# Pairwise bilinear products: W in one packed buffer with half-width loads, chunks aligned at their ends, one transposed x

## The chip, the cores and the metric

The kernel runs on one core of a Trainium2 chip. The metric is the device time of one execution in microseconds (us); of several executions the median is taken. Engines are called by the names of the profile: PE is TensorE (matmuls), PEld its weight loads, DVE is VectorE, ACT is ScalarE, POOL is GpSimd, SP is SyncE, which here only issues DMAs. A "tile" in this document is a tile of 128 batch rows unless it says otherwise.

## The reference

There are F = 32 fields of D = 64 features for each of 4,096 batch rows. For each of the 496 pairs of fields i < j there is one matrix W of 64 x 64. The output of a pair is field i times W, multiplied element by element with field j:

```python
i_idx, j_idx = np.triu_indices(32, k=1)
vi = inputs[:, i_idx, :]
vj = inputs[:, j_idx, :]
vdotw = jnp.einsum('bpd,pde->bpe', vi, W)
inter = vdotw * vj
return inter.reshape(B, -1)
```

All is float32. x is 33.6 MB, W 8.1 MB without padding, the output 520 MB.

## The kernel before, in words

The batch is cut into 32 tiles of 128 rows (the loop over t, L122). In each tile the 32 fields are taken as 16 pairs of neighbours: p stands for the fields 2p (even) and 2p + 1 (odd). Field i has `width[i]` = (31 - i) x 64 output columns, one 64-column block for each later field.

x of a tile is loaded by one DMA on ACT's queue (`load_x`, L80 to 83) into one of two buffers. PE needs it transposed, features on partitions: `transpose_x` (L97) makes eight 128 x 128 transposes into two PSUM banks and one ACT copy of them to xT. One xT tile holds all 16 pairs; for pair p, the even field lies on partitions 0 to 63 and the odd field on partitions 64 to 127. There are two xT buffers. The two halves of the next tile's xT are made at the pairs 5 and 6 of this tile (`PREFETCH_AT`, L133 to 136), ahead of those pairs' matmuls in PE's order.

W lies in HBM as 128 rows: rows 0 to 63 for even fields, rows 64 to 127 for odd fields, the odd ones padded by 64 columns so that both have the same width (16,384 columns in all). It is loaded once, by 16 DMAs on SP's queue, one per pair, each of 128 partitions, into 16 SBUF tiles (L113 to 116). The stores are issued from the same queue, behind these loads.

The products of a pair are cut into chunks of up to 512 columns from the left (L137). A chunk takes two PSUM banks out of a ring of eight (`take_banks`), one matmul goes into each (even field and odd field), and DVE multiplies both with x in one instruction of up to 1,024 columns (L155), whose sources and destination are two runs. Its x operand starts at two places, 64 columns apart, one for each field. Where the odd part is missing, or the padding would reach past the end of the group, DVE takes the two fields one by one (L164). Padding columns that L155 writes are overwritten by the following instruction.

DVE writes into a ring of 28,160 columns of SBUF. One tile has 31,744 output columns, in four groups (`STORES`): pairs 0 and 1 (7,552 columns), 2 and 3 (6,528), 4 to 6 (7,872), 7 to 15 (9,792). After each group SP issues one store of it (L170). A group that doesn't fit in the rest of the ring starts again at column 0. The first DVE instruction that writes over a part of the ring waits for the store that still reads it.

The order on each engine is the order of the program. The framework adds the waits, by the regions that are read and written, also inside one large buffer.

Of the kernel before, what the change touches and what calls it, by code (L numbers as in the profile page):

```python
# [1 line left out]

# [6 lines left out]

F32 = mybir.dt.float32  # L10
ALU = mybir.AluOpType

P = 128
BANK = 512
BANKS = 8
CHUNK = BANK

STORES = [[0, 1], [2, 3], [4, 5, 6], [7, 8, 9, 10, 11, 12, 13, 14, 15]]
PREFETCH_AT = [5, 6]
RING = 28160  # L20


@with_exitstack
def pair_bilinear_kernel(
    ctx: ExitStack,
    tc: tile.TileContext,
    x: bass.AP,
    w: bass.AP,
    out: bass.AP,
    F: int,  # L30
    D: int,
):

    nc = tc.nc
    B = x.shape[0]
    NT = B // P
    NPR = F // 2

    width = [(F - 1 - i) * D for i in range(F)]
    off = [sum(width[:i]) for i in range(F)]
    woff = [sum(width[0 : 2 * p : 2]) for p in range(NPR)]  # L60
    store_w = [sum(width[2 * p] + width[2 * p + 1] for p in g) for g in STORES]

    const = ctx.enter_context(tc.tile_pool(name="const", bufs=1))
    xtpool = ctx.enter_context(tc.tile_pool(name="xT", bufs=2))
    psum = ctx.enter_context(tc.tile_pool(name="ps", bufs=1, space=bass.MemoryType.PSUM))

    ident = const.tile([P, P], F32, tag="ident", name="ident")
    make_identity(nc, ident)

    def runs(tl, a, b, n):  # L70

        ap = tl[:, a : a + n]
        return bass.AP(ap.tensor, ap.offset, [list(ap.ap[0]), [b - a, 2], list(ap.ap[1])])


    xbuf = [const.tile([P, (F + 1) * D], F32, tag=f"x{b}", name=f"x{b}") for b in range(2)]
    for xb in xbuf:
        nc.gpsimd.memset(xb[:, F * D :], 0.0)  # L78

    def load_x(t):  # L80
        xt = xbuf[t % 2]
        nc.scalar.dma_start(out=xt[:, : F * D], in_=x[ts(t, P), :])
        return xt

    pring = psum.tile([P, BANKS * BANK], F32, tag="pring", name="pring")
    bank = 0

    def take_banks(n):

        nonlocal bank  # L90
        if bank + n > BANKS:
            bank = 0
        got = pring[:, bank * BANK : (bank + n) * BANK]
        bank = (bank + n) % BANKS
        return got

    def transpose_x(xT, t, xt, g):  # L97

        n = 2 * BANK // P
        pt = take_banks(2)  # L100
        for c in range(n):
            nc.tensor.transpose(pt[:, ts(c, P)], xt[:, ts(n * g + c, P)], ident)  # L102
        nc.scalar.copy(xT[:, ts(g, 2 * BANK)], pt)  # L103

    def new_xT(t):
        return xtpool.tile([P, NPR * P], F32, tag="xT", name=f"xT_{t}")

    ring = const.tile([P, RING], F32, tag="ring", name="ring")
    at = 0
    xs = {0: load_x(0)}  # L110

    w_sb = []
    for p in range(NPR):  # L113
        wp = const.tile([P, width[2 * p]], F32, tag=f"w{p}", name=f"w{p}")
        nc.sync.dma_start(out=wp, in_=w[:, woff[p] : woff[p] + width[2 * p]])
        w_sb.append(wp)

    xTs = {0: new_xT(0)}
    for g in range(2):
        transpose_x(xTs[0], 0, xs[0], g)  # L120

    for t in range(NT):  # L122
        xt, xT = xs.pop(t), xTs.pop(t)
        if t + 1 < NT:
            xs[t + 1] = load_x(t + 1)
        for s, group in enumerate(STORES):
            if at + store_w[s] > RING:
                at = 0
            osb = ring[:, at : at + store_w[s]]
            at += store_w[s]  # L130
            o0 = off[2 * group[0]]
            for p in group:
                if t + 1 < NT and p in PREFETCH_AT:  # L133
                    if t + 1 not in xTs:
                        xTs[t + 1] = new_xT(t + 1)
                    transpose_x(xTs[t + 1], t + 1, xs[t + 1], PREFETCH_AT.index(p))
                for c0 in range(0, width[2 * p], CHUNK):  # L137
                    n = [max(0, min(CHUNK, width[2 * p + h] - c0)) for h in range(2)]
                    half = -(-n[0] // BANK) * BANK
                    pm = take_banks(2 * half // BANK)  # L140
                    for b0 in range(0, n[0], BANK):
                        b1 = min(b0 + BANK, n[0])
                        for h in range(2):
                            if b0 < n[h]:
                                nc.tensor.matmul(  # L145
                                    pm[:, h * half + b0 : h * half + b1],
                                    xT[h * D : (h + 1) * D, ts(p, P)],
                                    w_sb[p][h * D : (h + 1) * D, c0 + b0 : c0 + b1],
                                    start=True,
                                    stop=True,  # L150
                                )
                    o = [off[2 * p + h] - o0 + c0 for h in range(2)]
                    xj = [(2 * p + h + 1) * D + c0 for h in range(2)]
                    if n[1] > half - BANK and o[1] + n[0] <= store_w[s]:
                        nc.vector.tensor_tensor(  # L155
                            runs(osb, o[0], o[1], n[0]),
                            runs(pm, 0, half, n[0]),
                            runs(xt, xj[0], xj[1], n[0]),
                            ALU.mult,
                        )  # L160
                    else:
                        for h in range(2):
                            if n[h]:
                                nc.vector.tensor_tensor(  # L164
                                    osb[:, o[h] : o[h] + n[h]],
                                    pm[:, h * half : h * half + n[h]],
                                    xt[:, xj[h] : xj[h] + n[h]],
                                    ALU.mult,
                                )
            nc.sync.dma_start(out=out[ts(t, P), o0 : o0 + store_w[s]], in_=osb)  # L170


# [33 lines left out]
```

## Time and profile before

| what | value |
|---|---|
| median of 3 runs | 1337.88 us (1337.68 to 1337.98) |
| the profiled execution's own time | 1337.58 us |
| its span (first to last instruction) | 1335.8 us |
| PE busy | 1154.1 us (86%) |
| DVE busy | 1199.1 us (90%) |
| ACT busy | 66.1 us (5%) |
| moved by DMA | 562.88 MB, 421 GB/s over the span |
| of it written to HBM | 520.09 MB |
| clock granted to TensorE | 0.971 of full speed |

The profile is of one execution. Its page shows the busy time of each engine, then the span in 40 equal slices with the busy share in tenths (9 is 90% or more), the DMA queues, and groups of instructions: line, engine, operation, destination and sources, shape and count, then busy time and the mean duration of one in ns, and last the idle time before them with what ended it. Queue q1 is SP's, q10 is ACT's. Busy times of matmuls are modelled, since matmuls are pipelined. Beside the page, the trace answers questions on waits and on single stretches of the span, and it keeps a record of each DMA packet: queue, start, duration and size.

### The profile page before, as it was taken

The numbers are of one execution on the slowest core, as the hardware profiler recorded it, in microseconds if no ns is written. First come the engines' busy times: TensorE is split into PE (matmuls) and PEld (weight loads), VectorE is DVE, ScalarE is ACT, GpSimd is POOL, SyncE is SP. The second block draws the span as 40 slices with busy tenths as digits, with TensorE's granted clock in tenths as the row PEclk, the third lists the DMA queues.
The fourth block names the chain that finished last, engine by engine and source line by source line (L and its number), as shares of the span: only waits on it lengthen the run. The fifth ranks groups of instructions, "written<-read, shape, count | busy, mean of one in ns | idle before, by whom it ended". The sixth has DMA issues, their size and how long they took to land. (4 is left out here: it accounts for less than half of the span.)

```text
span 1335.8 us, 13084 instructions
## 1 busy us (share of the span) xinstructions
PE 1154.1 (86%) x5376; PEld 529.9 (40%) x5376; DVE 1199.1 (90%) x1344; ACT 66.1 (5%) x65; POOL 0.9 (0%) x8
## 2 busy tenths in 40 slices
PE   7898898988888889898888898898988888888883
PEld 3343343433343444344334444343443333333331
DVE  5999898999899999899999899989988989999994
ACT  1000000000000000000000000000000000000000
POOL 0000000000000000000000000000000000000000
PEclk9999999899999999999999999999999999999997
DMA  9999999999999999999999999999999999999998
GB/s 392 435 426 431 436 408 434 415 426 431 419 417 425 428 429 416 418 424 420 424 436 419 418 421 426 424 426 421 418 430 414 426 423 413 424 427 430 418 420 370
DMA packets 25403, 562.88 MB, mean 421 GB/s; under 512 B 2944, under 2 KB 3328, under 8 KB 4864
## 3 DMA queue, kind: packets, MB, share of 16 engines
q1 hardware_dynamic: 20736, 528.49, 92.6%
q10 hardware_dynamic: 4608, 33.56, 6.0%
q8 instruction: 42, 0.69, 0.2%
q14 instruction: 17, 0.14, 0.0%
HBM read 41.94 MB, written 520.09 MB: 421 GB/s over the span
## 5 line engine op out<-in xcount | busy, mean ns | idle before, releaser
L155 DVE TENSOR_TENSOR ring<-pring,x 128x1024 f32<-128x1024 f32 (+3 forms) x1088 | 1154.2, 1107 | 116.9 <-DMA out_dram<-ring 68.0
L145 PE MATMUL pring<-w,xT 64*128 64x512 f32 (+4 forms) x4864 | 1087.8, 563 | 132.3 <-DVE ring L155 127.9
L145 PEld LDWEIGHTS pring<-w,xT 64*128 64x128 f32 x4864 | 472.9, 192 | 721.4 <-DVE ring L155 611.7
L103 ACT COPY xT<-pring 128x1024 f32<-128x1024 f32 x64 | 64.8, 1012 | 1197.1 <-PE pring L102 1197.1
L102 PE MATMUL pring<-ident,x 128*128 128x128 f32 x512 | 71.5, 285 | 30.7 <-DMA x<-in_x_dram 30.3
L102 PEld LDWEIGHTS pring<-ident,x 128*128 128x128 f32 x512 | 57.0, 144 | 65.6 <-issue 65.6
L164 DVE TENSOR_TENSOR ring<-pring,x 128x64 f32<-128x64 f32 (+4 forms) x256 | 70.9, 297 | 3.3
L103 ACT ACT_TABLE_LOAD x1 | 1.3, 1283 | 1.7 <-PEq L198 1.7
masks.py:199 POOL TENSOR_SCALAR_AFFINE_SELECT ident<-ident 128x128 f32<-128x128 f32 x1 | 0.3, 292 | 0.0
L78 POOL MEMSET x<- 128x64 f32 x2 | 0.2, 152 | 0.0
masks.py:197 POOL MEMSET ident<- 128x128 f32 x1 | 0.2, 204 | 0.3 <-POOLq L198 0.3
L198 POOL MEMSET const-bfloat16-1.0<- 128x1 bf16 x1 | 0.1, 101 | 0.0
L198 POOL MEMSET const-uint8-127<- 128x1 uint8 x1 | 0.1, 101 | 0.0
L198 POOL MEMSET const-float32-0.0<- 128x1 f32 x1 | 0.1, 98 | 0.2 <-issue 0.2
L198 POOL MEMSET const-float32-1.0<- 128x1 f32 x1 | 0.1, 98 | 0.0
## 6 DMA issues: line engine op xcount, KB each, us to landing
out_dram<-ring SPq DMA_DIRECT2D x32, 4896.0 KB, 18.6
out_dram<-ring SPq DMA_DIRECT2D x32, 3936.0 KB, 17.4
out_dram<-ring SPq DMA_DIRECT2D x32, 3776.0 KB, 19.0
out_dram<-ring SPq DMA_DIRECT2D x32, 3264.0 KB, 19.4
x<-in_x_dram ACTq DMA_DIRECT2D x32, 1024.0 KB, 17.8
w<-in_w_dram SPq DMA_DIRECT2D x1, 992.0 KB, 7.5
w<-in_w_dram SPq DMA_DIRECT2D x1, 928.0 KB, 11.8
w<-in_w_dram SPq DMA_DIRECT2D x1, 864.0 KB, 13.4
```

The lines of the kernel that those rows point to most:

```text
L78: nc.gpsimd.memset(xb[:, F * D :], 0.0)
L102: nc.tensor.transpose(pt[:, ts(c, P)], xt[:, ts(n * g + c, P)], ident)
L103: nc.scalar.copy(xT[:, ts(g, 2 * BANK)], pt)
L145: nc.tensor.matmul(pm[:, h * half + b0 : h * half + b1], xT[h * D : (h + 1) * D, ts(p, P)], w_sb[p][h * D : (h + 1) * D, c0 + b0 : c0 + b1 ...
L155: nc.vector.tensor_tensor(runs(osb, o[0], o[1], n[0]), runs(pm, 0, half, n[0]), runs(xt, xj[0], xj[1], n[0]), ALU.mult,)
L164: nc.vector.tensor_tensor(osb[:, o[h] : o[h] + n[h]], pm[:, h * half : h * half + n[h]], xt[:, xj[h] : xj[h] + n[h]], ALU.mult,)
L198: nc = bacc.Bacc("TRN2", target_bir_lowering=False, num_devices=1)
```

## The change

W is stored in one SBUF buffer of 16,384 columns, without the padding. In HBM the odd fields' half starts with 64 columns of zeros, and behind them the odd fields follow one another without gaps; the last 960 columns of that half are never loaded. The load is cut into five groups of pairs (`LOADS`: pair 0, pair 1, pairs 2 and 3, 4 to 6, 7 to 15), and each group into two DMAs, one for the partitions 0 to 63 and one for 64 to 127: ten DMAs of 64 partitions, with rows of 7,168 to 20,736 bytes.

Chunks are now aligned at their right end: the first chunk of a pair is the short one. The odd field's columns are counted one block further left, so that one chunk of both fields needs the same columns of x. DVE's x operand then reads one run twice (a step of 0). In the first chunk of a pair the odd field's first 64 columns are no result of it; they fall on the last block of the even field's output and are overwritten by the pair's last chunk. A pair that has a single chunk (the pairs 12 to 15) is taken field by field.

There is one xT buffer. The second half of this tile's xT is made at pair 3 of the tile, the first half of the next tile's at pair 9. Before the first tile only one half is made. The x buffers lose their 64 columns of zeros and with them two memsets.

```diff
-CHUNK = BANK
 
 STORES = [[0, 1], [2, 3], [4, 5, 6], [7, 8, 9, 10, 11, 12, 13, 14, 15]]
-PREFETCH_AT = [5, 6]
+
+LOADS = [[0], [1], [2, 3], [4, 5, 6], [7, 8, 9, 10, 11, 12, 13, 14, 15]]
+
+FIRST_HALF_AT, SECOND_HALF_AT = 9, 3
...
-    woff = [sum(width[0 : 2 * p : 2]) for p in range(NPR)]
+    woff = [i % 2 * D + sum(width[i % 2 : i : 2]) for i in range(F)]
...
-    xtpool = ctx.enter_context(tc.tile_pool(name="xT", bufs=2))
+    xT = const.tile([P, NPR * P], F32, tag="xT", name="xT")
...
-    w_sb = []
-    for p in range(NPR):
-        wp = const.tile([P, width[2 * p]], F32, tag=f"w{p}", name=f"w{p}")
-        nc.sync.dma_start(out=wp, in_=w[:, woff[p] : woff[p] + width[2 * p]])
-        w_sb.append(wp)
+    load_x(0)
+    w_sb = const.tile([P, sum(width[0::2])], F32, tag="w", name="w")
+    for g in LOADS:
+        for h in range(2):
+            a = woff[2 * g[0] + h]
+            b = woff[2 * g[-1] + h] + width[2 * g[-1] + h]
+            if h and g is LOADS[0]:
+                a -= D
+            nc.sync.dma_start(
+                out=w_sb[h * D : (h + 1) * D, a:b], in_=w[h * D : (h + 1) * D, a:b]
+            )
 
-    xTs = {0: new_xT(0)}
-    for g in range(2):
-        transpose_x(xTs[0], 0, xs[0], g)
-
+    transpose_x(xbuf[0], 0)
...
-                if t + 1 < NT and p in PREFETCH_AT:
-                    if t + 1 not in xTs:
-                        xTs[t + 1] = new_xT(t + 1)
-                    transpose_x(xTs[t + 1], t + 1, xs[t + 1], PREFETCH_AT.index(p))
-                for c0 in range(0, width[2 * p], CHUNK):
...
+                if p == SECOND_HALF_AT:
+                    transpose_x(xt, 1)
+                if p == FIRST_HALF_AT and t + 1 < NT:
+                    transpose_x(xbuf[(t + 1) % 2], 0)
+                first = (width[2 * p] - 1) % BANK + 1
+                for c1 in range(first, width[2 * p] + 1, BANK):
+                    n = first if c1 == first else BANK
+                    c0 = c1 - n
+                    odd = width[2 * p + 1] and c1 > D
+                    pm = take_banks(2)
+                    for h in range(1 + bool(odd)):
+                        a = woff[2 * p + h] + c0 - h * D
+                        nc.tensor.matmul(
+                            pm[:, h * BANK : h * BANK + n],
+                            xT[h * D : (h + 1) * D, ts(p, P)],
+                            w_sb[h * D : (h + 1) * D, a : a + n],
+                            start=True,
+                            stop=True,
+                        )
+                    xj = xt[:, (2 * p + 1) * D + c0 : (2 * p + 1) * D + c1]
+                    o = [off[2 * p + h] - o0 + c0 - h * D for h in range(2)]
+                    if odd and (c0 or c1 < width[2 * p]):
                         nc.vector.tensor_tensor(
-                            runs(osb, o[0], o[1], n[0]),
-                            runs(pm, 0, half, n[0]),
-                            runs(xt, xj[0], xj[1], n[0]),
+                            runs(osb, o[0], o[1], n),
+                            runs(pm, 0, BANK, n),
+                            bass.AP(xj.tensor, xj.offset, [xj.ap[0], [0, 2], xj.ap[1]]),
                             ALU.mult,
                         )
                     else:
-                        for h in range(2):
-                            if n[h]:
...
+                        for h in range(1 + bool(odd)):
+                            nc.vector.tensor_tensor(
+                                osb[:, o[h] + h * D : o[h] + n],
+                                pm[:, h * (BANK + D) : h * BANK + n],
+                                xj[:, h * D :],
+                                ALU.mult,
+                            )
```

## The prediction

> **What bounds the kernel now.** I read the page first: the busy shares and slices say which resource has no holes.
>
> ```profile
> span 1335.8 us, 13084 instructions
> ...
> DVE  5999898999899999899999899989988989999994
> ...
> DMA  9999999999999999999999999999999999999998
> GB/s 392 435 426 431 436 408 434 415 426 431 419 417 425 428 429 416 418 424 420 424 436 419 418 421 426 424 426 421 418 430 414 426 423 413 424 427 430 418 420 370
> DMA packets 25403, 562.88 MB, mean 421 GB/s; under 512 B 2944, under 2 KB 3328, under 8 KB 4864
> ...
> q1 hardware_dynamic: 20736, 528.49, 92.6%
> q10 hardware_dynamic: 4608, 33.56, 6.0%
> ```
>
> The DMA row has no slice below 9 before the last, and q1 (W loads and stores) with q10 (x) fill 98.6% of the 16 engines' span. VectorE (DVE) is busy for 90%. So I asked who waits for whom; each row gives the total, the times and the longest wait.
>
> ```profile
> DVE ring L155 <- DMA out_dram<-ring: 68.0, 35, 3.0
> DVE ring L155 <- PE pring L145: 16.7, 7, 13.6
> ```
>
> DVE waits about once a tile for a store to free ring space; for TensorE (PE) it waits 13.6 us at the start and 3.1 us in all the rest. The store queue is the bound. Next come stretches of the span: the W load, one steady tile (cut between two returns of DVE from that wait), and the tail after the last store's issue at 1319.3.
>
> ```profile
> 4.00:12.00 8.00, 3.46 (x16) 3.28 (x16) 0.00 (x0) 1.01 (x1) 0.00 (x0) 1.00 1.01 425
> 12.00:20.00 8.00, 7.67 (x35) 3.47 (x36) 6.28 (x6) 1.01 (x1) 0.00 (x0) 1.00 1.01 419
> 561.45:602.46 41.01, 36.63 (x171) 17.72 (x169) 37.48 (x42) 2.35 (x3) 0.00 (x0) 0.96 0.99 423
> 1319.30:1330.20 10.90, 0.00 (x0) 0.00 (x0) 0.00 (x0) 0.00 (x0) 0.00 (x0) 0.54 0.96 410
> ```
>
> The last two columns are DMA share and GB/s. The W load already runs at the rate of the steady tile, so it takes its bytes' worth of a full resource. The trace's packet records give each packet's size and duration: 300 ns for 7,936 B, 309 ns for 8,192 B, 1,448 ns for 39,168 B. That is 27.2 B/ns for one engine plus 8.2 ns a packet; 16 such engines give 435 GB/s. W's packets run from 1.75 to 28.23 us; the first store packet starts at 27.57, though the first store was issued at 24.7. Stores sit behind W in the same queue, so every microsecond that W takes longer moves all stores.
>
> One steady tile takes 41.0 us. An engine's own share is 8 packets of each store (1,448, 1,166, 1,119 and 968 ns) and 8 of x (309 ns): 40.1 us. The engine that ends last lags the others by about 3 us in each store. Others idle about 0.6 us a tile, but the last one has no hole.
>
> [...] All DMAs of the kernel before span 128 partitions, so no row here shows a half-width one[...].
>
> **The change part by part.**
>
> (1) W as ten half-width loads. Before, one engine carries 16,384 columns x 4 B x 8 rows = 524,288 B of W and 2 x 65,536 B of x: 655,360 / 27.2 = 24.1 us, plus 144 packets x 8.2 ns = 1.2, together 25.3 us; the records show 25.8 up to the first store packet. After, W has 16,384 columns in the lower half and 15,424 in the upper. Two bounds:
> Fast bound, engines limit: 31,808 x 4 B x 4 rows = 508,928 B an engine, 15,360 B less (0.56 us), and 88 data packets fewer (0.72 us): -1.3 us.
> Slow bound[...]: lower 16,384 x 4 x 64 B over 8 x 27.2 GB/s = 19.3 us; upper 15,424 likewise 18.1; 37.4 us, with 40 packet overheads 37.8. Before it was 19.3 + 1.05 = 20.3. So +17.4 us. [...]
> I take the slow side[...]: +15.6 us.
>
> (2) What a late W does to compute. DVE consumes W at 64 rows x 4 B per output column. A 1024-column product takes 1,217 ns, so 215 GB/s, about the half-width rate (218): compute waits only for whole loads. x0 shares the queues and lands some 2 us later. The largest load, pairs 7 to 15, lands near 46 us, while DVE reaches pair 7 at about 45; there it must wait anyway for store 0 (ring space), which starts at 45 and is in memory at 56. DVE then needs 12.2 us for group 7 to 15, done at 68; a store's first packet comes about 2 us after DVE's end, and the engines are free at 45 + 9.0 + 7.8 + 9.4 = 71. Hidden with about 1 us to spare; without that cover, up to 1 us more.
>
> (3) DVE's chunking, by shape:
>
> ```profile
> L155 DVE TENSOR_TENSOR ring<-pring,x 128x896 f32<-128x896 f32 x128 | 138.1, 1079 | 0.0
> L155 DVE TENSOR_TENSOR ring<-pring,x 128x640 f32<-128x640 f32 x96 | 78.5, 818 | 3.7 <-DVE ring L155 0.5
> L155 DVE TENSOR_TENSOR ring<-pring,x 128x384 f32<-128x384 f32 x96 | 52.8, 550 | 3.2
> L164 DVE TENSOR_TENSOR ring<-pring,x 128x320 f32<-128x320 f32 x32 | 15.3, 480 | 0.0
> L164 DVE TENSOR_TENSOR ring<-pring,x 128x256 f32<-128x256 f32 x32 | 13.2, 411 | 0.0
> L164 DVE TENSOR_TENSOR ring<-pring,x 128x192 f32<-128x192 f32 x32 | 11.1, 347 | 0.0
> L164 DVE TENSOR_TENSOR ring<-pring,x 128x128 f32<-128x128 f32 x32 | 8.9, 279 | 0.0
> ```
>
> Pairs 1 and 6 merge their last two products: 480 + 411 becomes 818 (-73 ns), 347 + 279 becomes 550 (-76). Pairs 12, 13, 14 split: 1,079 becomes 448 + 384 columns, 616 (1.043 ns a column between 64 and 1024) + 550 = 1,166 (+87); 818 becomes 480 + 411 (+73); 550 becomes 347 + 279 (+76). Sum +0.09 us a tile, 43 products for 42, and +0.16 in the two groups between the ring wait and the last store's issue. Cover: the lagging engine ends the third store about 3 us after the fourth store's first packet starts (0.16 against 3). Uncovered it would be 32 x 0.16 = 5 us. A source read twice (step 0) I cost at nothing; the trace has no such row, and if it cost 5% (61 ns on each of some 31 products, 1.9 us a tile) most of it would still be covered.
>
> (4) One xT, transposes at pairs 3 and 9. Matmuls and transposes keep their numbers. PE no longer waits for x at pair 5 (30.3 us in all, 8.5 of it the start), PE time that DVE never felt. What is queued behind a transpose on PE is the next products; PSUM holds four chunks, and 8 transposes take 1.09 us. The ACT copy overwrites a half whose readers stand earlier in PE's own order. The first product needs one ACT copy and 8 transposes, where 16 stood ahead of it: about 0.5 us sooner, hidden because stores wait for W. Two memsets go, hidden.
>
> (5) SP has six DMA issues fewer; x stays on ACT's queue at the same place. The tail is unchanged: stores end the kernel.
>
> Sum: 1337.58 us is the profiled execution's own time, with a span of 1335.8; the median of the runs is 1337.88, 0.3 us above it. 1337.58 + 15.6 + 0.0 to 0.5 for (2) = 1353.4; as a median I say 1353.5, +1.2%.
>
> **Rivals.** 0.2% (2.7 us) is about what a measurement of this kernel can tell from no change.
> A. [...] (chance 0.68): 1350 to 1357 with more or less overlap; slower.
> B. [...] regain half or more (0.09): 1341 to 1350; slower. [...]
> C. Not slower: an engine's own 27.2 B/ns is the limit[...], and fewer, longer packets save 1.3 us: 1336.5 (0.16; the last 0.03 of it for a gain over 2.7 us). It decides as soon as W flows at more than 8.14 MB / 23 us = 354 GB/s. [...]
> D. W is hidden or harmless, but DVE becomes the pacemaker of the ring (0.03): +5 us, 1343. Against: the 3 us of cover.
> E. [...] partial loads stall compute (0.04): above 1358.
>
> **How the numbers follow.** The likeliest is A, 1353.5. A, B and D make slower 0.80, E adds 0.04: 0.84; same 0.13; faster 0.03. A to B and D alone would leave out a little more than 2 in 10 (C, E and A's edges), so the range takes in C: 1336 to 1358; A's own is 1350 to 1357.
>
> **What would show it.** Right: W's packets of about 8 KB take near 600 ns where they took 300, GB/s in the stretch 12 to 20 falls from 419 to 220 to 260, the first store packet comes at 42 to 45 us, and from there the period is again 41.0 us. Step 3 is wrong if the period per tile grows, step 4 if DVE waits for PE by more than a few us after the start, step 2 if the DMA share has a hole between 45 and 75 us. Wrong altogether (C): W's stretch holds 419 GB/s or more and stores begin at 26 to 27 us.

## The result and the profile after

The changed kernel takes 1356.48 us (median of 4 runs, 1355.73 to 1358.39) against 1337.78 us (4 runs, 1337.66 to 1337.98): a ratio of 1.0142, 95% interval 1.0124 to 1.0159. The forecast was 1353.5 us, with a range of 1336 to 1358, and slower with a chance of 0.84. The profiled execution took 1357.03 us with a span of 1355.2 us, 19.4 us more than the span before.

The page of the kernel after, in the same rows as were shown of the page before:

```profile
span 1355.2 us, 13139 instructions
...
DVE  3698999888988888998888989889988889898894
...
DMA  9999999999999999999999999999999999999998
GB/s 226 349 432 429 436 426 423 431 424 421 422 414 421 432 425 422 414 422 423 433 419 420 420 420 439 421 413 428 427 418 421 413 424 424 414 422 432 426 419 359
DMA packets 23900, 562.64 MB, mean 415 GB/s; under 512 B 2720, under 2 KB 2720, under 8 KB 2976
...
q1 hardware_dynamic: 19232, 528.25, 92.5%
q10 hardware_dynamic: 4608, 33.56, 6.1%
```

A slice is 34 us. The whole difference stands in the first two: 226 and 349 GB/s where 392 and 435 stood; from the third on the rates are those of before. The row of busy shares says nothing of it: the DMA engines are just as "busy" with little more than half the bytes in the first slice. The kernel after moves fewer bytes (562.64 for 562.88 MB) in fewer packets (23,900 for 25,403), and takes longer.

Stretches of the span after (share and GB/s last):

```profile
4.00:12.00 8.00, 3.69 (x10) 2.07 (x10) 0.00 (x0) 1.01 (x1) 0.00 (x0) 1.00 1.03 271
12.00:20.00 8.00, 5.16 (x15) 3.32 (x16) 2.32 (x2) 0.00 (x0) 0.00 (x0) 1.00 1.06 232
20.00:28.00 8.00, 5.34 (x27) 3.89 (x25) 6.81 (x7) 0.00 (x0) 0.00 (x0) 0.91 1.03 220
28.00:36.00 8.00, 8.00 (x35) 4.76 (x31) 6.16 (x7) 1.01 (x1) 0.00 (x0) 0.88 0.95 203
36.00:44.00 8.00, 7.99 (x37) 4.36 (x36) 8.00 (x10) 0.00 (x0) 0.00 (x0) 1.00 1.08 226
561.45:602.46 41.01, 36.45 (x172) 17.23 (x170) 37.12 (x44) 2.03 (x2) 0.00 (x0) 0.96 0.99 422
```

Before, 12 to 20 us moved 419 GB/s. Here DMA moves 203 to 232 GB/s from 12 to 44 us, nearly all of it W, and the steady stretch (here the same times of the span as before, so a cut at another place of the tile) is back at 422. Who waits for whom after:

```profile
DVE ring L157 <- DMA out_dram<-ring: 107.3, 40, 4.3
DVE ring L157 <- PE pring L147: 24.9, 11, 16.8
DVE ring L165 <- DMA out_dram<-ring: 10.8, 1, 10.8
PE pring L147 <- DMA w<-in_w_dram: 10.4, 4, 2.9
```

The last row has no counterpart before: PE waits four times in the first tile for W. The third row is DVE's wait for the first store, at 46 to 57 us. DVE's waits for ring space grew, which is no cost: DVE needs less time now (1183.0 us busy for 1199.1; step 3 below says why) and waits for the same stores.

From the packet records, in us, with the mean period of a tile (last packet of the fourth store, from tile 4 to tile 30):

| | W's last packet ends | first store packet starts | period |
|---|---|---|---|
| before | 28.2 | 27.57 | 40.92 |
| after | 47.6 | 46.38 | 40.92 |

The first store comes 18.8 us later, 26 steady periods take the same time, and the span is 19.4 us longer.

### The profile page after: what moved, and what is told of

The parts are those of the page before. It is cut to its first block, busy times and chain, and to the rows that moved or that the text cites. A ratio compares the mean times of both kernels' runs of the same rounds, so it can differ in the third digit from the quotient of the medians.

```text
span 1355.2 us, 13139 instructions
## 1 busy us (share of the span) xinstructions
PE 1170.5 (86%) x5376; PEld 556.5 (41%) x5376; DVE 1183.0 (87%) x1376; ACT 66.1 (5%) x65; POOL 0.7 (0%) x6
## 2 busy tenths in 40 slices
DMA packets 23900, 562.64 MB, mean 415 GB/s; under 512 B 2720, under 2 KB 2720, under 8 KB 2976
## 4 chain that ended last, share of the span: by engine, by line
DMA 48%; DVE 38%; issue 10%; PE 3%; DVEq 0%; SPq 0%
DMA out_dram<-ring 47%; DVE ring L157 32%; DVE ring L165 5%; PE pring L147 3%; DMA w<-in_w_dram 1%; DVEq L157 0%; PE pring L105 0%; SPq L119 0%; DVEq L196 0%; DVEq L165 0%
## 5 line engine op out<-in xcount | busy, mean ns | idle before, releaser
L147 PE MATMUL pring<-w,xT 64*128 64x512 f32 (+4 forms) x4864 | 1107.6, 570 | 158.8 <-DVE ring L157 137.3
L157 DVE TENSOR_TENSOR ring<-pring,x 128x1024 f32<-128x1024 f32 (+3 forms) x1056 | 1103.8, 1107 | 143.1 <-DMA out_dram<-ring 107.3
L147 PEld LDWEIGHTS pring<-w,xT 64*128 64x128 f32 x4864 | 500.3, 195 | 722.8 <-DVE ring L157 520.3
L165 DVE TENSOR_TENSOR ring<-pring,x 128x64 f32<-128x64 f32 (+3 forms) x320 | 97.6, 355 | 11.4 <-DMA out_dram<-ring 10.8
```

Of the source, the lines that this page charges most:

```text
L147: nc.tensor.matmul(pm[:, h * BANK : h * BANK + n], xT[h * D : (h + 1) * D, ts(p, P)], w_sb[h * D : (h + 1) * D, a : a + n], start=True, st ...
L157: nc.vector.tensor_tensor(runs(osb, o[0], o[1], n), runs(pm, 0, BANK, n), bass.AP(xj.tensor, xj.offset, [xj.ap[0], [0, 2], xj.ap[1]]), ALU ...
L165: nc.vector.tensor_tensor(osb[:, o[h] + h * D : o[h] + n], pm[:, h * (BANK + D) : h * BANK + n], xj[:, h * D :], ALU.mult,)
```

## The experiments

**Half width alone, in the kernel before.** Theory A of the expectations is rival A of the forecast: W is slow because each of its loads covers one half of the partitions.

```diff
-        nc.sync.dma_start(out=wp, in_=w[:, woff[p] : woff[p] + width[2 * p]])
+        for h in range(2):
+            nc.sync.dma_start(
+                out=wp[h * D : (h + 1) * D, :],
+                in_=w[h * D : (h + 1) * D, woff[p] : woff[p] + width[2 * p]],
+            )
```

> The kernel before with each of its 16 W loads cut into two DMAs, partitions 0 to 63 and 64 to 127; nothing else is changed. If the half width is the cause (theory A[...]): W's packets take twice as long (7,936 B in 530 to 610 ns instead of 300), the first store packet comes near 46 us instead of 27.6, and the time is 1355 to 1359 us. If the packed layout, the long rows, the chunking or the single xT is the cause: 1337 to 1340 us.

Measured: 1356.38 us against 1337.86; ratio 1.0139 (1.0125 to 1.0153). The first store packet starts at 46.35 us, the period is 40.92 us. The packets of 7,936 B, the first pair's, have a median of 495 ns, a little under the 530 to 610 expected, where they took 300; those of 7,424 B, sent after them, have 553 ns, where they took 281. The stretch from 12 to 20 us:

```profile
12.00:20.00 8.00, 5.46 (x17) 2.63 (x18) 2.62 (x3) 0.00 (x0) 0.00 (x0) 1.00 1.01 225
```

This one edit gives the whole loss. Layout, row length, chunking and xT are those of before, so they aren't needed for it.

**Full width in the changed kernel.**

```diff
-        for h in range(2):
-            a = woff[2 * g[0] + h]
-            b = woff[2 * g[-1] + h] + width[2 * g[-1] + h]
-            if h and g is LOADS[0]:
-                a -= D
-            nc.sync.dma_start(
-                out=w_sb[h * D : (h + 1) * D, a:b], in_=w[h * D : (h + 1) * D, a:b]
-            )
+        a = woff[2 * g[0]]
+        b = woff[2 * g[-1]] + width[2 * g[-1]]
+        nc.sync.dma_start(out=w_sb[:, a:b], in_=w[:, a:b])
```

> The changed kernel with W loaded by five DMAs of 128 partitions, one per group of pairs, at the even fields' column bounds; layout, chunks and xT stay as changed. Theory A: packets at 26 to 27 B/ns, first store packet at 26 to 27 us, and 1336.0 to 1337.0 us, a little below the kernel before since there are fewer packets. If the rest of the change costs something (chunking on the ring's cycle, transposes): above 1338 us, with a period per tile above 40.92 us. If the layout is the cause: it stays at 1356 us.

Measured: 1338.07 us against 1337.86 (13 and 17 runs); ratio 1.0002 (0.9994 to 1.0010). The stretches of the span from 4 to 28 us:

```profile
4.00:12.00 8.00, 2.34 (x10) 1.97 (x12) 0.00 (x0) 1.01 (x1) 0.00 (x0) 1.00 1.02 430
12.00:20.00 8.00, 8.00 (x30) 3.52 (x30) 5.62 (x6) 0.00 (x0) 0.00 (x0) 1.00 1.02 434
20.00:28.00 8.00, 7.76 (x38) 3.24 (x36) 8.00 (x9) 1.01 (x1) 0.00 (x0) 1.00 1.05 419
```

DMA moves 419 to 434 GB/s again, and W's packets of 7,936 B take 300 ns. The rest of the change, all of it, is worth nothing that can be measured: period 40.94 us, first store packet at 27.37 us, 0.2 us sooner than before. The gain of 1.3 us that I had put on fewer and longer packets did not come. Of it 0.56 us can't come here, since full-width loads carry the unused columns; of the other 0.7 us, the packets' summed durations show 0.4 (25.9 us an engine for W and the first two tiles of x, 26.3 before). Why no more than 0.2 of it reached the first store was not settled. Since this version equals the kernel before within its interval, no version here beats both.

**64 partitions in the middle.** Each load is cut into three, to tell the number of partitions from their place: 64 partitions that lie half below and half above partition 64, then the two outer quarters. That the middle ones would run at the full rate was an assumption of mine that no trace had shown.

```diff
-        nc.sync.dma_start(out=w_sb[:, a:b], in_=w[:, a:b])
+        for r0, r1 in [(32, 96), (0, 32), (96, 128)]:
+            nc.sync.dma_start(out=w_sb[r0:r1, a:b], in_=w[r0:r1, a:b])
```

> As the full-width version, but each group's load is cut into three DMAs by partitions: 32 to 95, 0 to 31, 96 to 127. Theory A[...]: the DMA of 64 partitions in the middle [...] run at 26 to 27 B/ns, and those of the two outer DMAs at about 13 B/ns; W takes 9.6 + 19.3 us plus a little, the first store packet comes at 36 to 38 us, the time is 1346 to 1348 us. Rival (any DMA of 64 or fewer partitions is slow, because each engine gets only 4 rows or 2): all packets slow, 1356 us or more.

Measured: 1348.21 us, 0.2 above the range expected; ratio 1.0078 (1.0064 to 1.0092). The first store packet starts at 37.79 us. Taken in order of start, the packets of the last group show the parts: the first 64 packets of 20,736 B (the middle) have a median of 779 ns, 26.6 B/ns; the next 32 and the last 32 (the outer parts) 1,569 and 1,526 ns, 13.2 and 13.6 B/ns. The stretches hold both kinds:

```profile
12.00:20.00 8.00, 8.00 (x25) 4.84 (x25) 4.12 (x4) 0.00 (x0) 0.00 (x0) 1.00 1.03 293
20.00:28.00 8.00, 7.64 (x26) 3.19 (x24) 6.74 (x8) 0.00 (x0) 0.00 (x0) 1.00 1.03 278
```

So it isn't the number of partitions that makes a load slow, but which partitions it covers. Of 20,736 B a packet, 64 partitions from 32 on run at the full rate (779 ns; 775 for the same size at full width); 32 partitions from 0 on run at half of it (1,569 ns), as 64 from 0 on do in the kernel after (1,615 ns in the median). A limit for each side of partition 64 would fit this; the trace shows the durations, not what limits them. Half of W at half rate costs 10.2 us at the first store, a little over half of the 18.8.

**Both halves at once, from two queues.**

```diff
-            nc.sync.dma_start(
+            (nc.scalar if h else nc.sync).dma_start(
                 out=w_sb[h * D : (h + 1) * D, a:b], in_=w[h * D : (h + 1) * D, a:b]
             )
```

> The changed kernel with the upper halves of W (partitions 64 to 127) issued from ACT's queue and the lower halves from SP's, so that each engine has a packet of both halves to choose from. If engines go through both queues in step (all on one half at a time): no gain, 1354 to 1358 us. If an engine's two queues overlap[...]: W regains most of its rate, first store packet at 27 to 33 us, 1337 to 1343 us. [...] I expect 1350, between the two and nearer to no gain.

Measured: 1352.36 us; ratio 1.0106 (1.0090 to 1.0121). W's last packet ends at 40.0 us instead of 47.6 and the first store packet starts at 39.15 us, 7.2 us sooner. But the order of issue now also puts the second tile of x behind W on ACT's queue, which takes its packets out of this stage and brings them back later. Added up for each engine, x's packets ahead of the first store fall from 7.5 to 3.1 us, and only W's own from 37.4 to 34.7: 14.7 B/ns for 13.6, 8% more. In the stretches the DMA share stays near 1 (1.00 and 1.06), as it would with one packet an engine at a time:

```profile
20.00:28.00 8.00, 7.75 (x38) 3.19 (x36) 8.00 (x9) 0.00 (x0) 0.00 (x0) 1.00 1.00 228
28.00:36.00 8.00, 7.79 (x40) 3.69 (x38) 8.00 (x10) 1.01 (x1) 0.00 (x0) 1.00 1.06 240
```

In the packet records the sizes of the two halves take turns: 16 packets of 20,736 B start between 35.1 and 35.9 us, then 16 of 18,432 B between 36.5 and 37.3. So here an engine takes the packets of its two queues in turn and not side by side, and the engines stay nearly in step: most are on the same half at the same time. One wait is new, but it doesn't set the first store:

```profile
ACT L106 <- DMA w<-in_w_dram: 14.0, 1, 14.0
```

ACT issues its fifth W load only when an earlier one has landed, and its first copy to xT stands behind that issue. Even so, SP had issued the first store at 27.6 us, and its first packet came only when W's last ones left the engines. Since x has moved, the time doesn't measure the overlap alone; by the packets, two queues raise W's rate by some 8%, and full width nearly doubles it.

**DVE's cover.** In the full-width version, one product done three times:

```diff
                     if odd and (c0 or c1 < width[2 * p]):
-                        nc.vector.tensor_tensor(
+                        for _ in range(3 if p == 8 and n == BANK else 1):
+                            nc.vector.tensor_tensor(
```

> The full-width version with one 1,024-column product of pair 8 done three times: two more of 1,217 ns, 2.4 us more for DVE in every tile, between the wait for ring space and the fourth store's issue. If the last DMA engine paces the kernel and DVE has 3 to 4 us of cover a tile (step 3): within 1 us of the full-width version's 1338.1 us, with the same period of 40.9 us. If DVE and the ring's cycle are already the pacemaker (rival D): 32 x 2.4 = 78 us more, near 1416 us; a part of it if the cover is smaller than I read it.

Measured: 1340.15 us (17 runs) against 1337.58 (20); ratio 1.0019 (1.0012 to 1.0026), where the full-width version had 1.0002. First the full-width version's steady stretch, then this one's (the tile cut at another place), then this one's waits and, last, the wait for stores in the full-width version:

```profile
561.45:602.46 41.01, 35.86 (x168) 16.23 (x168) 36.87 (x43) 2.02 (x2) 0.00 (x0) 1.00 0.99 422
```

```profile
561.45:602.46 41.01, 36.47 (x170) 16.84 (x168) 39.09 (x46) 2.02 (x2) 0.00 (x0) 0.96 0.97 412
```

```profile
DVE ring L153 <- DMA out_dram<-ring: 34.5, 25, 2.3
DVE ring L153 <- PE pring L142: 25.0, 30, 13.5
```

```profile
DVE ring L152 <- DMA out_dram<-ring: 103.8, 37, 4.1
```

78 us of DVE work cost about 2.3 us, more than the 1 us that I had allowed. Most of them went into DVE's wait for stores (103.8 us down to 34.5), and the period stays at 40.94 us. The lagging engine ended the third store about 4.0 us after the fourth store's first packet in most tiles; now it is 0.6 to 2.0. The cover is real, and mostly used up here. Rival D falls.

**Half width beside stores.** In the full-width version, x instead of W:

```diff
-        nc.scalar.dma_start(out=xbuf[t % 2], in_=x[ts(t, P), :])
+        for h in range(2):
+            nc.scalar.dma_start(
+                out=xbuf[t % 2][h * D : (h + 1) * D, :],
+                in_=x[t * P + h * D : t * P + (h + 1) * D, :],
+            )
```

> The full-width version with every load of x cut into two DMAs, partitions 0 to 63 and 64 to 127. It asks what a half-width load costs where it runs beside stores[...]. If a slow packet holds its DMA engine: 8 packets of 309 ns become about 620, 2.5 us a tile, 30 to 32 tiles, near 1413 us. If an engine goes on with a store packet meanwhile[...]: 1338 to 1345 us. I expect the first, perhaps softened[...]: 1380 to 1413 us.

Measured: 1350.02 us; ratio 1.0091 (1.0074 to 1.0108). Neither expectation held. More than half of it is the start: the first store packet comes at 34.10 us for 27.37, and while x's halves run beside W, W's packets of 13,312 B have a median of 852 ns for 498. In the steady part the period grows from 40.94 to 41.10 us, 0.16 x 30 = 5 us. The x packets there have a median of 309 ns and a mean of 318, for 309 and 311 at full width: beside stores most of them take no longer than at full width. A part of the cost stands in the stores instead: their packets of 39,168 B have a mean of 1,519 ns after the start for 1,483. That a half-width load is slow only while many engines write into the same half is my reading of these durations; no run showed it by itself.

**Which engine lags.** Again in the full-width version. I assumed that this split of x leaves one engine without x; that was not shown, since the packet records name no engine:

```diff
-        nc.scalar.dma_start(out=xbuf[t % 2], in_=x[ts(t, P), :])
+        for r0, r1 in [(0, 120), (120, 128)]:
+            nc.scalar.dma_start(
+                out=xbuf[t % 2][r0:r1, :], in_=x[t * P + r0 : t * P + r1, :]
+            )
```

> The full-width version with every load of x cut into 120 rows and 8 rows. It asks which DMA engine is the one that ends last. [...] If that is the lagging one, its 40.9 us a tile fall to about 40.3 to 40.5[...] and the time to 1318 to 1326 us; if another one lags: 1338 us or up to 10 us more.

Measured: 1357.89 us; ratio 1.0154 (1.0137 to 1.0171), twice the loss that I had allowed. The period grows to 41.30 us, by 0.36. If the lagging engine carried no x here, the period would have fallen. 0.36 us is about one x packet of 309 ns more a tile, but the stores' packets of 39,168 B took longer as well (1,508 ns in the mean for 1,483, 0.2 us for eight of them); which engine lags, and why, stays open. The start was slower too: the first tile's last store ends 7.4 us later than in the full-width version, and W's first packets took 495 ns and x's 507, where they took 300 and 309 in the kernel before: this split of x slows both at the start.

## Why the prediction was right, step by step

**The bound** was right. With stores as the bound, the delay of the first store packet (18.8 us) comes back in the span (19.4), and no later stage recovers it.

**Step 1** was right in its mechanism and too small. I took +15.6 us, between bounds of -1.3 and +17.4. Measured are 18.8 at the first store, outside the upper bound: its packet came at 46.38 us, where I had named 42 to 45. W's packets of about 8 KB took 527 to 564 ns in the median, where I had named near 600; the stretch from 12 to 20 us moved 232 GB/s, inside my 220 to 260. What the packets took, added up for each engine until the first store, in us:

| | forecast before | measured before | forecast after | measured after |
|---|---|---|---|---|
| W's packets | 20.3 | 21.3 | 37.8 (slow bound) | 37.4 |
| x's packets, two tiles | 5.0 | 5.0 | 5.0 | 7.5 |

Together they grew by 18.6 us, which is nearly all of the 18.8. W gives 16.1 of it and x 2.5. The term that I had put at nothing is x: its packets, still at full width, take turns with W's half-width ones, and those sent after 5.5 us have a mean of 558 ns, where they took 309. W's term, 16.1 us, is near the 15.6 of the forecast partly by luck, since two errors cancel in part: W before took 1.0 us more than I had reckoned, and I had gone below the slow bound of 17.4 because I took the two halves to overlap, which no trace had shown and which is nearly absent from one queue. In the packet records of the last three groups each half's first packet starts only 0.6 us before the other half's last packet ends: all engines go from half to half nearly together. The half rate itself, which the slow bound takes (8 x 27.2 GB/s, where 16 engines at that rate give 435), was right: 508,928 B in 37.4 us are 13.6 B/ns over all of W, though the late packets run a little below it (20,736 B in a mean of 1,573 ns are 13.2). That loads of one half run at it was the assumption that decided the forecast; no trace of the kernel before showed it.

**Step 2**: compute was covered, with nothing to spare. The timeline of DVE around the fourth group of the first tile:

```profile
39.30 6.94 DVE L157 TENSOR_TENSOR ring<-pring,x 128x1024 f32<-128x1024 f32 x7
57.07 0.23 DVE L165 TENSOR_TENSOR ring<-pring,x 128x64 f32<-128x64 f32 x1 [10.83 <-DMA out_dram<-ring]
57.21 4.67 DVE L157 TENSOR_TENSOR ring<-pring,x 128x1024 f32<-128x1024 f32 x4
62.73 0.82 DVE L157 TENSOR_TENSOR ring<-pring,x 128x640 f32<-128x640 f32 x1 [0.85 <-PE pring L147]
64.34 3.05 DVE L157 TENSOR_TENSOR ring<-pring,x 128x1024 f32<-128x1024 f32 x3 [0.78 <-PE pring L147]
...
68.56 2.40 DVE L165 TENSOR_TENSOR ring<-pring,x 128x448 f32<-128x448 f32 x7
```

DVE waits for the first store until 57.1 (forecast 56) and ends the group at 70.9, not 68: it waits twice for PE (0.85 and 0.78 us), and starts 1 us later. The fourth store's first packet starts at 72.56 us, the moment the first engine leaves the third store (72.56). There is no hole, but the spare microsecond was gone. The step allowed about 2 us from DVE's end to a store's first packet; here it was 1.6, and for the fourth stores of all tiles 0.9 in the median.

**Step 3** was right in its prices and in the period. The shapes that it priced, after, and last the large product before:

```profile
L165 DVE TENSOR_TENSOR ring<-pring,x 128x448 f32<-128x448 f32 x32 | 19.7, 615 | 0.0
L165 DVE TENSOR_TENSOR ring<-pring,x 128x384 f32<-128x384 f32 x32 | 17.5, 548 | 0.0
...
L157 DVE TENSOR_TENSOR ring<-pring,x 128x1024 f32<-128x1024 f32 x768 | 902.4, 1217 | 15.7 <-PE pring L147 4.9
```

```profile
L155 DVE TENSOR_TENSOR ring<-pring,x 128x1024 f32<-128x1024 f32 x768 | 903.2, 1217 | 110.0 <-DMA out_dram<-ring 68.0 <-PE pring L145 16.7 <-PE pring L102 2.5
```

448 columns take 615 ns (616 forecast), and a product that reads x twice takes the same 1,217 ns as one that reads two places. The durations of all products add up to 1283.0 us for 1280.2, +0.09 us a tile as forecast. What the sum left out is the time between products. Before, 310 gaps of some 0.1 us took 32.0 us; after, 108 take 11.6, and in the trace neighbouring products overlap by 100.0 us in all instead of 81.1. So DVE's work on a tile became about 1.1 us shorter and not 0.09 longer, and DVE spends that in its waits for stores. The kernel before with half-width loads still has 311 such gaps, so they go with the rest of the change; why they went wasn't tested. The period did not grow, and the experiment with a longer DVE shows the cover.

**Step 4** was right: after 90 us DVE waits 2.9 us for PE in all, for 5.6 before (7.7 in the full-width version, all small beside more than 100 us of waits for stores there).

**Step 5** was right in that nothing of it shows; it was not tried by itself.

**The rivals.** C, full rate, is excluded by the packets. B, in which W regains half or more of the lost rate, is too: in the last three groups not one packet comes near full rate (the fastest of 20,736 B took 1,427 ns, where it takes 775 at full width). E's stall of compute was near but did not come.

## What to carry to other kernels

Load across all 128 partitions, or across a range that lies half below and half above partition 64 (26.6 B/ns an engine here for 32 to 95, 13.6 for one side alone), when loads stand alone at the start of a store-bound kernel: each microsecond there moves every store. When you price a slow load, price also the full-width loads that take turns with it: here they gave 2.5 of 18.6 us. Read GB/s beside the DMA's busy share, since a full share with half the bytes is how the slow load looked here (a share of 1.06 at 232 GB/s, where 1.01 stood at 419). Beside a stream of stores the half-width load of x cost little (0.16 us a tile), so width mattered most where loads were by themselves.

## What the runs showed of the hardware

- A DMA of 64 partitions ran at full rate at partitions 32 to 95 (26.6 B/ns an engine) and at half rate at 0 to 63 or 64 to 127 (13.6 B/ns over all of W, 12.8 to 13.0 in the median of its late packets). The half rate I had assumed; that half-width x costs only 0.16 us a tile beside stores I had not.
- A full-width load that took turns with half-width ones was slowed too: x's packets took 558 ns for 309.
- Loads of the two halves from two queues ran at 14.7 B/ns, not 13.6: a second queue hardly took the engines out of step.
- In each store one DMA engine ends 3 to 4.5 us after most of the others (I read the last packets as one engine's, since the last two of the fourth store end 1.49 us apart before and 1.45 after, in the median, about one packet of 1,448 ns), in every version but the one with the longer DVE, where it is 1.4 to 1.9. The period is 40.9 us where an engine's packets add up to 40.1. That this engine sets the period is my reading, and the cause of its lag stays open.
